# A graph kernel's edge sort: a running table in four classes of columns, table joins in three batches, and ranks by one comparison per step

## The chip, the cores and the metric

The kernel runs on one core of one Trainium2 chip. The time is that of one execution on the device in microseconds, the median of several runs. The core's engines are TensorE (PE in the profile; PEld is its weight load), VectorE (DVE), ScalarE (ACT), GpSimd (POOL) and SyncE (SP, which only issues DMAs here). Each takes its own instructions in order and waits for the others by semaphores.

## What is computed

A graph of 6250 nodes with 128 features and 100,000 edges goes through two layers, each followed by a residual sum and a layer norm. The edges come sorted by their destination, not by their source.

```python
# layer 0: attention over edges, 8 heads of 16
q, k, v = (x @ W.T + b for W, b in ((Wq, bq), (Wk, bk), (Wv, bv)))
scores = sum(q[src] * k[dest], per head) / sqrt(16) + attention_mask
weights = softmax of scores over the edges with the same src
out = segment_sum(v[src] * weights, dest) @ Wo.T + bo
# layer 1: a message per edge
h = silu(concat(x[src], x[dest], edge_features) @ eW1 + eb1)
agg = segment_sum(silu(h @ eW2 + eb2), src)
x = silu(concat(x, agg) @ nW1 + nb1) @ nW2 + nb2
```

The softmax runs over edges of one source, so the kernel first sorts the edges by source, on the chip.

## The kernel before

**Layout.** The edges stand in 784 columns of 128 (a column is one edge per partition). 16 columns make a step: 49 steps. The steps form three regions (`REG`): steps 0 to 8, steps 9 to 12, and the rest, the far region; the first two are the near regions, whose destinations are all in a narrow band. Each region is sorted on its own into a table `xs` in DRAM. A source node is a pair (block of 128 nodes, of which there are 49; place in the block).

**The counting sort.** `hist_steps` counts the edges of every node: for each column, a one-hot of the place (`lo1`, L229) times a one-hot of the block (`hi1`, L233) is accumulated on TensorE into `hist` (128 places x 49 blocks). `places` turns the counts of a region into the first position of each node (`st_b`: three parts whose sum is exact in bf16).

**One step of the sort** (loop at L897; its parts are interleaved by hand there, and a scheduler may move instructions further along each engine's queue, within the dependences). `prep_loads` issues the loads of the next step. `prep_hot` makes `hit` (L780, the one-hot of the place, transposed) and `lo1`, `hi1`. `prep_rank` makes `ohd` (L786) and the rank: how many edges with the same source stand earlier in the same column. `sk` holds, for each partition, the 127 keys before its own, for 16 columns; a comparison with the own key, with a sum, gives the rank of one column (L790), 16 times a step. `chain` (two halves of 8 columns) keeps the running table `base` in PSUM: how many edges of each node have passed. For each column, ScalarE copies `base` to `cs` (L805), TensorE adds the column to `base` (L806), and three matmuls with `hit` look up first position plus passed edges for the column's own nodes (`look`, L808). `pick` selects the right block (L822, L824); `send` adds the rank (L835), forms the position (L837) and scatters 8 columns, one indirect DMA each, from GpSimd (helper at L133). What is scattered is `stg`, a buffer of three copies, filled by `spread_k` (L817, the keys' projection spread by `ohd`) and `heads` (L828, L829). The first write to a copy (L828) waits until the scatters of three steps before have landed.

**Work beside the sort.** `between`, called after each half step, pulls a few pieces of other work: in steps 1 to 7 the histogram of the other regions and projections; at the end of step 7 `places` for regions 1 and 2; from step 9 on weights and projections, three pieces a time; then the near regions' scores, four pieces a time (`near_scores`, L704). That takes each near region's 16-column chunks from `xs` (fetch, turn, score, soft, stat: 14 pieces) and sums maxima and sums of exponentials per node into `stat_r`. At a region's end the sums are joined into `near_o`: for 4 blocks at a time, transposes (L725), a reduction (L728), and `pooled` (L692), which merges maxima and sums; each group is one piece. Behind the last region's joins `stat_r` is cleared (L739).

**Behind the sort.** `fast` (L939) handles the far region in the same way, reading `xs` from its first load on, then computes messages (scatters into `xmsg`), sums by destination, and runs layer 1.

Of the kernel before, what the change touches and what calls it, by code (L numbers as in the profile page):

```python
# [18 lines left out]
P = 128  # L19
# [13 lines left out]
AC = sum(AS)  # L33
BC = NC - AC
AT = AC * UC
REG = ((0, 9), (9, 4), (AC, BC))
KEYS = ((0, AS[0]), (AS[0], NC - AS[0]))
WT = (2, 1, 8)
# [20 lines left out]
def tile_gnn(  # L59
# [120 lines left out]
    def bank():  # L180
        return gps.tile([P, 512], F32, name="ps")
# [34 lines left out]

    def halves(r):
        cs = slice(KEYS[r][0] * UC, (KEYS[r][0] + KEYS[r][1]) * UC)
        part = ks.tile([P, 2, KEYS[r][1] * UC], I32, name=f"part{r}")
        nc.vector.tensor_single_scalar(part[:, 0], kc[r], P - 1, ALU.bitwise_and)  # L220
        nc.vector.tensor_copy(lo_c[:, cs], part[:, 0])
        nc.vector.tensor_single_scalar(part[:, 1], kc[r], 7, ALU.logical_shift_right)
        nc.vector.tensor_copy(hi_c[:, cs], part[:, 1])

    def onehots(c, pool, bufs=None):

# [118 lines left out]
            yield  # L345

    kps = sort.enter_context(tc.tile_pool(name="ksetp", bufs=1, space=PSUM))
    hist = kps.tile([P, len(REG), NB], F32, name="hist")
# [12 lines left out]

    def places(r):

        cnts.append(kp.tile([P, NB], F32, name=f"cnt{r}"))
        nc.vector.tensor_copy(cnts[r], hist[:, r, :])
        sums = bank()[:, :3 * NB].rearrange("p (a b) -> p a b", b=NB)
        nc.tensor.matmul(sums[:, 0, :], ones_f, cnts[r], start=True, stop=True)
        nc.tensor.matmul(sums[:, 1, :], after, cnts[r], start=True, stop=True)

        many = kp.tile([P, 1], F32, name=f"many{r}")  # L370
        nc.vector.tensor_reduce(many, cnts[r], AX.X, ALU.max)
        nc.vector.tensor_single_scalar(many, many, float(2 * P), ALU.is_gt)
# [6 lines left out]
        st_i = kp.tile([P, 4, NB], I32, name=f"st_i{r}")  # L379
        nc.vector.tensor_add(st_i[:, 3, :], pre[r], sums[:, 1, :])  # L380
        nc.vector.tensor_scalar(st_i[:, 0, :], st_i[:, 3, :], 9, 9, ALU.logical_shift_right, ALU.logical_shift_left)
        nc.vector.tensor_single_scalar(st_i[:, 1, :], st_i[:, 3, :], 510, ALU.bitwise_and)
        nc.vector.tensor_single_scalar(st_i[:, 2, :], st_i[:, 3, :], 1, ALU.bitwise_and)
        st_b.append(kp.tile([P, 3, NB], BF16, name=f"st_b{r}"))
        nc.vector.tensor_copy(st_b[r], st_i[:, :3, :])
# [306 lines left out]
    def pooled(o, z, sp, nwin, k):  # L692

        m, s = z[:, :, :, 0:8], z[:, :, :, 8:16]
        d = sp.tile([P, nwin, k, 8], F32, name=f"pd{k}{nwin}")
        nc.vector.tensor_scalar(d, s, 0.0, -BIG, ALU.is_equal, ALU.mult)
        nc.vector.tensor_add(d, d, m)
        nc.vector.tensor_reduce(o[:, :, 0:8], d.rearrange("p w k h -> p w h k"), AX.X, ALU.max)
        nc.vector.tensor_sub(d, d, o[:, :, None, 0:8].to_broadcast([P, nwin, k, 8]))
        nc.scalar.activation(d, d, AF.Exp)  # L700
        nc.vector.tensor_mul(d, d, s)
        nc.vector.tensor_reduce(o[:, :, 8:16], d.rearrange("p w k h -> p w h k"), AX.X, ALU.add)

    def near_scores():  # L704

        for r in range(FAR):
            with ExitStack() as own:
# [13 lines left out]
                for j0 in range(0, NB, 4):  # L721
                    m = min(4, NB - j0)
                    x = bank()
                    for i in range(m):
                        nc.tensor.transpose(x[:, i * 96:(i + 1) * 96],  # L725
                                            sums_of["src"][:96, (j0 + i) * P:(j0 + i + 1) * P], ident[:96, :96])
                    z = sp.tile([P, 4, 3, 16], F32, name="z3")
                    nc.vector.tensor_reduce(z[:, :m, 0:2].rearrange("p w a v -> p w (a v)"),  # L728
                                            x[:, :m * 96].rearrange("p (w k v) -> p w v k", k=3, v=32), AX.X, ALU.add)
                    o = sums_of["near"][:, j0:j0 + m]  # L730
# [4 lines left out]
                    some = sp.tile([P, 4, 8], F32, name="some")  # L735
                    nc.vector.tensor_single_scalar(some[:, :m], o[:, :, 8:16], 0.0, ALU.is_gt)
                    nc.vector.tensor_mul(o[:, :, 0:8], o[:, :, 0:8], some[:, :m])
                    yield
        nc.vector.memset(sums_of["src"], 0.0)  # L739
        yield  # L740
# [6 lines left out]
    base = cps.tile([P, NB], F32, name="base")  # L747
    kreg, work = {}, {}

    def region(c):  # L750
# [32 lines left out]
    def prep_rank(c):  # L783
        w = work[c]
        w["ohd"] = bw.tile([P, UC, P], BF16, name="ohd")
        nc.vector.tensor_scalar(w["ohd"], w["drow"], iota_p, None, ALU.is_equal)  # L786
        w["rank"] = bw.tile([P, UC], F32, name="rank")
        for j in range(UC):
            junk = bw.tile([P, 127], BF16, name="junk")
            nc.vector.tensor_scalar(junk, w["sk"][:, :, j], meta[:, c * UC + j, 0:1], 0.0, ALU.is_equal, ALU.add,  # L790
                                    accum_out=w["rank"][:, j:j + 1])

    def chain(c, h):
        w = work[c]
        r, cr = region(c)
        if h == 0:
            w["stg"] = bw.tile([P, UC, XW], F32, name="stg", bufs=3)
            w["pos"] = bw.tile([P, UC], F32, name="pos")
            if cr == 0:
                nc.tensor.matmul(base, ident_b, st_b[r][:, 2, :], start=True, stop=False, skip_group_check=True)  # L800
        w["look"] = lps.tile([P, 8, NB], F32, name="look", bufs=2)
        for j in range(8 * h, 8 * h + 8):
            lo, hi = (w[k][:, j // 4, :, j % 4] for k in ("lo1", "hi1"))
            cs = bw.tile([P, NB], BF16, name="cs", bufs=4)
            nc.scalar.copy(cs, base)  # L805
            nc.tensor.matmul(base, lo, hi, start=False, stop=False, skip_group_check=True)  # L806
# [24 lines left out]
    def send(c, h):  # L831
        w, hs = work[c], slice(8 * h, 8 * h + 8)
        r, _ = region(c)
        pos = w["pos"][:, hs]
        nc.vector.tensor_add(pos, pos, w["rank"][:, hs])  # L835
        posi = bw.tile([P, 8], I32, name="posi", bufs=6)
# [1206 lines left out]
```

## Time and profile before

| | |
|---|---|
| median of 3 runs | 3164.53 us (3162.35 to 3166.09) |
| the profiled execution | 3162.1 us |
| its span, first to last instruction | 3160.3 us |
| first scatter of the sort starts | 50.5 us |
| last scatter of the sort ends | 1219.8 us |
| busy in the span | PE 2308.0, DVE 2085.9, ACT 870.7, POOL 2066.0 us |
| granted TensorE clock, 50 to 436, 436 to 1220, behind that | 0.67, 0.63, 0.87 |

In a line of a group of instructions stand the line of the kernel, engine, operation, tiles (written<-read) and count; after the bar the busy time in us and the mean of one in ns; after the next bar the engine's idle time just before these instructions, and what ended most of it ("issue" is a wait for nothing that the profile shows). In the timeline the columns are start, duration, engine, line, operation, and in brackets the idle time before it. In the view of waits they are the total, the number of waits and the longest.

### The profile page before, as it was taken

Reading aid. Unit: us, or ns where it says so; the run is one execution under the profiler, and the core shown is the slowest. Engines: PE = TensorE matmul, PEld = TensorE weight load, DVE = VectorE, ACT = ScalarE, POOL = GpSimd, SP = SyncE. Lnnn points to the kernel's source line nnn. Section 1 sums busy time; section 2 is a strip of 40 time slices with the busy share of each in tenths; the row PEclk is TensorE's granted clock in tenths of the full one; section 3 lists DMA queues with packets and bytes.
Section 4 is the critical chain, followed back from the end, with each engine's and each line's share of the span. In section 5 each row is a group of like instructions: output and inputs, shape, how many; then the busy total and the mean of one; then the engine's idle time right before and its main releaser. Section 6 shows DMA issues by size and latency. Waiting matters only on the chain. (4 is left out here: it accounts for less than half of the span.)

```text
span 3160.3 us, 64246 instructions
## 1 busy us (share of the span) xinstructions
PE 2308.0 (73%) x22329; PEld 1875.0 (59%) x22412; DVE 2085.9 (66%) x6242; ACT 870.7 (28%) x2740; POOL 2066.0 (65%) x1993
## 2 busy tenths in 40 slices
PE   7767875555656532667778768644987999999998
PEld 5555545445545521556667657543975777777776
DVE  8886447676788762667778768634994555555564
ACT  3324433233323311222222222100042333333333
POOL 3877776677667653255777775775037777777774
PEclk9666667666666655778888878776998999999999
DMA  7855768566648614555665665325845444444452
GB/s 233 185 155 149 201 196 251 160 215 210 182 134 253 198 49 125 157 161 142 178 177 171 179 181 149 90 80 193 294 142 152 133 134 122 125 114 129 133 160 61
DMA packets 480741, 509.83 MB, mean 161 GB/s; under 512 B 150742, under 2 KB 403465, under 8 KB 475798
## 3 DMA queue, kind: packets, MB, share of 16 engines
q1 hardware_dynamic: 378644, 341.49, 37.8%
q0 software_dynamic: 61952, 132.22, 13.6%
q10 hardware_dynamic: 39810, 31.91, 3.4%
q8 instruction: 179, 2.93, 0.4%
q14 instruction: 156, 1.28, 0.1%
HBM read 380.69 MB, written 124.69 MB: 160 GB/s over the span
## 5 line engine op out<-in xcount | busy, mean ns | idle before, releaser
L133 POOL DMA_INDIRECT xs<-stg,posi x784 | 832.1, 1061 | 381.6 <-issue 207.3
L133 POOL DMA_INDIRECT xmsg<-msg,at x576 | 594.5, 1032 | 341.2 <-issue 139.1
L125 POOL DMA_INDIRECT bt<-b_tab,dsti x576 | 572.5, 994 | 175.4 <-issue 136.7
L806 PE MATMUL base<-hi,lo 128*128 128x49 bf16 x784 | 169.0, 216 | 214.1 <-ACT cs L805 175.7
L790 DVE TENSOR_SCALAR_CACHE_REDUCE junk<-sk,meta 128x127 bf16<-128x127 int16 x784 | 303.2, 436 | 9.1 <-DMA sk<-skew 9.1
L1294 DVE TENSOR_TENSOR fe<-po,b_sb 128x512 f32<-128x512 f32 x196 | 135.2, 690 | 241.2 <-PE po L1292 235.0
L808 PEld LDWEIGHTS <-hit 128*128 128x128 bf16 x2352 | 142.3, 114 | 230.8 <-issue 208.8
L815 PE MATMUL kx<-kw,ohd 128*128 128x128 bf16 x2352 | 239.8, 267 | 29.8 <-ACT stg L817 24.4
L805 ACT CAST cs<-base 128x49 bf16<-128x49 f32 x784 | 160.5, 205 | 312.7 <-PE base L806 247.8
L815 PEld LDWEIGHTS <-ohd 128*128 128x128 bf16 x2352 | 196.3, 123 | 59.2 <-issue 37.4
L1292 PEld LDWEIGHTS po<-w_sb,ht 128*128 128x128 f32 x1568 | 204.8, 193 | 26.7 <-issue 5.2
L610 PEld LDWEIGHTS <-oht 128*128 128x128 bf16 x2352 | 189.0, 121 | 42.7 <-DVE oht L597 28.5
L1313 PE MATMUL ps<-ohf,fe 128*128 128x128 f32 x1568 | 208.6, 276 | 6.8 <-ACT fe L1295 6.8
L1292 PE MATMUL po<-w_sb,ht 128*128 128x128 f32 x1568 | 210.9, 277 | 2.0 <-ACT ht L1286 0.7
L1313 PEld LDWEIGHTS ps<-ohf,fe 128*128 128x128 f32 x1568 | 191.1, 192 | 8.1 <-ACT fe L1295 8.0
L1295 ACT ACTIVATE fe<-fe 128x512 f32<-128x512 f32 x196 | 123.5, 630 | 230.9 <-DVE fe L1294 230.7
L808 PE MATMUL look<-st_b,hit 128*128 128x49 bf16 x1568 | 159.3, 206 | 35.2 <-DVE sel L822 27.5
L1154 PE MATMUL ps<-ohd,mt 128*128 128x128 f32 x1152 | 135.1, 280 | 66.2 <-DMA mt<-xmsg 61.7
L1286 ACT ACTIVATE ht<-pre 128x512 f32<-128x512 f32 x196 | 116.7, 596 | 241.0 <-PE pre L1282 221.9
L1154 PEld LDWEIGHTS ps<-ohd,mt 128*128 128x128 f32 x1152 | 132.7, 196 | 68.7 <-issue 60.2
L996 PE MATMUL qv<-vw,oht 128*128 128x128 bf16 x1728 | 137.7, 229 | 33.8 <-DVE msg L999 25.1
L610 PE MATMUL qv<-qw,oht 128*128 128x128 bf16 x1728 | 147.0, 255 | 18.1 <-DVE oht L597 13.7
(317 smaller groups left out, 5124.2 us busy)
## 6 DMA issues: line engine op xcount, KB each, us to landing
st<-xs SPq DMA_DIRECT2D x49, 1128.0 KB
srow<-slo_row SPq DMA_DIRECT2D x85, 512.0 KB
lob<-lob_row SPq DMA_DIRECT2D x49, 512.0 KB
drow<-dlo_row SPq DMA_DIRECT2D x49, 512.0 KB
sk<-skew SPq DMA_DIRECT2D x49, 508.0 KB
qw<-q_tab SPq DMA_DIRECT2D x208, 96.0 KB
aw<-a_tab SPq DMA_DIRECT2D x208, 96.0 KB
mt<-xmsg ACTq DMA_DIRECT2D x18, 1024.0 KB
```

The costliest lines, as they stand in the source:

```text
L125: nc.gpsimd.indirect_dma_start(out=dst, out_offset=None, in_=table, in_offset=bass.IndirectOffsetOnAxis(ap=idx, axis=0))
L133: apart(nc.gpsimd.indirect_dma_start(out=table, out_offset=bass.IndirectOffsetOnAxis(ap=idx, axis=0), in_=src, in_offset=None), group)
L610: nc.tensor.matmul(qe[:, i, :], w["oh"][:, 4 * q + i, :], w["qw"][:, (4 * q + i) // WT[r] % 8, k, :], start=(k == 0), stop=(k == 2))
L790: nc.vector.tensor_scalar(junk, w["sk"][:, :, j], meta[:, c * UC + j, 0:1], 0.0, ALU.is_equal, ALU.add, accum_out=w["rank"][:, j:j + 1])
L805: nc.scalar.copy(cs, base)
L806: nc.tensor.matmul(base, lo, hi, start=False, stop=False, skip_group_check=True)
L808: nc.tensor.matmul(w["look"][:, j - 8 * h, :], w["hit"][:, j, :], tab, start=(i == 0), stop=(i == 2))
L815: nc.tensor.matmul(kx[:, i, :], w["ohd"][:, 4 * q + i, :], w["kw"][:, q, a, :], start=(a == 0), stop=(a == 2))
L996: nc.tensor.matmul(ve[:, i, :], w["oh"][:, 4 * q + i, :], w["vw"][:, (4 * q + i) // WT[r], k, :F], start=(k == 0), stop=(k == 2))
L1154: nc.tensor.matmul(ps, mt[:, 4 * q + i, :], oh[:, i, :], start=(i == 0), stop=(i == 3))
L1292: nc.tensor.matmul(po[:, i, :], ht[:, i, :], cw["w2"], start=(i == 0), stop=(i == 3))
L1313: nc.tensor.matmul(ps[:, t % max(4, wt) // wt, :], fe_[:, t % 4, :], oh[:, t % 4, :], start=(t % wt == 0), stop=(t % wt == wt - 1))
```

## The change

- **Four classes.** Column j of a step belongs to class j mod 4. `hist` and `base` get 4 x 49 columns, one table per class; `st_b` holds a first position per node and class (a node's edges of class 0 first, then class 1, ...). The chain copies `base` once per 4 columns, adds the four columns to it, and then looks them up.
- **Ranks.** All 16 columns of `sk` are compared with the own keys in one operation, in place; the 127 rows are folded onto 63, then on 32, by two additions, and one sum over the rest gives the ranks.
- **Joins.** The reductions L728 stay in groups of 4 blocks, a piece each; `pooled` and what follows run for 17, 17 and 15 blocks, from a pool of their own, with single copies of their buffers. A region's join is 17 pieces now, 13 before.
- **Small ones.** `posi` has 8 copies for 6; `halves` uses one scratch tile.

```diff
-                nc.tensor.matmul(hist[:, r, :], lo1[:, t // 4, :, t % 4], hi1[:, t // 4, :, t % 4],
-                                 start=(c == 0 and t == 0), stop=(c == c0 + n - 1 and t == UC - 1),
+                nc.tensor.matmul(hist[:, t % KT, :], lo1[:, t // 4, :, t % 4], hi1[:, t // 4, :, t % 4],
+                                 start=(c == c0 and t == 0), stop=(c == c0 + n - 1 and t == UC - 1),
                                  skip_group_check=True)
+            if c == c0 + n - 1:
+                classes[r] = ks.tile([P, KT, NB], F32, name="classes", bufs=2)
+                nc.vector.tensor_copy(classes[r], hist)
...
-        nc.vector.tensor_copy(cnts[r], hist[:, r, :])
+        nc.vector.tensor_reduce(cnts[r], classes[r].rearrange("p k b -> p b k"), AX.X, ALU.add)
...
+        st_f = ks.tile([P, KT, NB], F32, name="st_f")
+        nc.vector.tensor_add(st_f[:, 0, :], pre[r], sums[:, 1, :])
+        for k in range(1, KT):
+            nc.vector.tensor_add(st_f[:, k, :], st_f[:, k - 1, :], classes[r][:, k - 1, :])
+        st_i = ks.tile([P, 4, KT, NB], I32, name="st_i")
+        nc.vector.tensor_copy(st_i[:, 3], st_f)
...
+                for b0 in range(0, NB, 17):
+                    nb = min(17, NB - b0)
+                    z = sp.tile([P, 17, 3, 16], F32, name="z3", bufs=1)
+                    for j0 in range(b0, b0 + nb, 4):
...
+                        yield
+                    o = sums_of["near"][:, b0:b0 + nb]
                     if r:
-                        nc.vector.tensor_copy(z[:, :m, 2], o)
-                    pooled(o, z[:, :m, :3 if r else 2], sp, m, 3 if r else 2)
+                        nc.scalar.copy(z[:, :nb, 2], o)
+                    pooled(o, z[:, :nb, :3 if r else 2], sp, nb, 3 if r else 2)
...
+        sk = w["sk"]
+        own = bw.tile([P, 1, UC], I16, name="own")
+        nc.vector.tensor_copy(own[:, 0, :], meta[:, c * UC:(c + 1) * UC, 0])
+        nc.vector.tensor_tensor(sk, sk, own.to_broadcast([P, 127, UC]), ALU.is_equal)
+        nc.vector.tensor_add(sk[:, 0:63, :], sk[:, 0:63, :], sk[:, 64:127, :])
+        nc.vector.tensor_add(sk[:, 0:32, :], sk[:, 0:32, :], sk[:, 32:64, :])
         w["rank"] = bw.tile([P, UC], F32, name="rank")
-        for j in range(UC):
-            junk = bw.tile([P, 127], BF16, name="junk")
-            nc.vector.tensor_scalar(junk, w["sk"][:, :, j], meta[:, c * UC + j, 0:1], 0.0, ALU.is_equal, ALU.add,
-                                    accum_out=w["rank"][:, j:j + 1])
+        nc.vector.tensor_reduce(w["rank"], sk[:, 0:32, :].rearrange("p k j -> p j k"), AX.X, ALU.add)
...
-        for j in range(8 * h, 8 * h + 8):
-            lo, hi = (w[k][:, j // 4, :, j % 4] for k in ("lo1", "hi1"))
-            cs = bw.tile([P, NB], BF16, name="cs", bufs=4)
+        for j0 in range(8 * h, 8 * h + 8, KT):
+            cs = bw.tile([P, KT, NB], BF16, name="cs", bufs=4)
             nc.scalar.copy(cs, base)
-            nc.tensor.matmul(base, lo, hi, start=False, stop=False, skip_group_check=True)
-            for i, tab in enumerate((st_b[r][:, 0, :], st_b[r][:, 1, :], cs)):
-                nc.tensor.matmul(w["look"][:, j - 8 * h, :], w["hit"][:, j, :], tab, start=(i == 0), stop=(i == 2))
+            for j in range(j0, j0 + KT):
+                lo, hi = (w[k][:, j // 4, :, j % 4] for k in ("lo1", "hi1"))
+                nc.tensor.matmul(base[:, j - j0, :], lo, hi, start=False, stop=False, skip_group_check=True)
+            for j in range(j0, j0 + KT):
+                k = j - j0
+                for i, tab in enumerate((st_b[r][:, 0, k, :], st_b[r][:, 1, k, :], cs[:, k, :])):
+                    nc.tensor.matmul(w["look"][:, j - 8 * h, :], w["hit"][:, j, :], tab, start=(i == 0),
+                                     stop=(i == 2))
```

In the changed kernel these lines are: comparison L806, additions L807 and L808, sum L810, copy of `base` L823, matmul into `base` L826 and `look` L830, `pick` L845 and L847, `posi` L860, scatters L134.

More of the change, by code (lines that the diff above doesn't have):

```diff
@@ L35 @@
 AT = AC * UC
+KT = 4
 REG = ((0, 9), (9, 4), (AC, BC))
@@ L218, in halves @@
         cs = slice(KEYS[r][0] * UC, (KEYS[r][0] + KEYS[r][1]) * UC)
[L219 to L223, printed above, removed]
+        part = ks.tile([P, KEYS[r][1] * UC], I32, name=f"part{r}")
+        nc.vector.tensor_single_scalar(part, kc[r], P - 1, ALU.bitwise_and)
+        nc.vector.tensor_copy(lo_c[:, cs], part)
+        nc.vector.tensor_single_scalar(part, kc[r], 7, ALU.logical_shift_right)
+        nc.vector.tensor_copy(hi_c[:, cs], part)
     def onehots(c, pool, bufs=None):
@@ L347, in tile_gnn @@
     kps = sort.enter_context(tc.tile_pool(name="ksetp", bufs=1, space=PSUM))
-    hist = kps.tile([P, len(REG), NB], F32, name="hist")
+    hist = kps.tile([P, KT, NB], F32, name="hist")
+    classes = {}
     def hist_steps(r):
@@ L377, in places @@
         nc.vector.tensor_sub(pre[r], upto, sums[:, 0, :])
[L379 to L385, printed above, removed]
+        st_f = ks.tile([P, KT, NB], F32, name="st_f")
[4 more added lines that the diff above has]
+        nc.vector.tensor_copy(st_i[:, 3], st_f)
+        nc.vector.tensor_scalar(st_i[:, 0], st_i[:, 3], 9, 9, ALU.logical_shift_right, ALU.logical_shift_left)
+        nc.vector.tensor_single_scalar(st_i[:, 1], st_i[:, 3], 510, ALU.bitwise_and)
+        nc.vector.tensor_single_scalar(st_i[:, 2], st_i[:, 3], 1, ALU.bitwise_and)
+        st_b.append(kp.tile([P, 3, KT, NB], BF16, name=f"st_b{r}"))
+        nc.vector.tensor_copy(st_b[r], st_i[:, :3])
         few.append(kp.tile([P, 1], F32, name=f"few{r}"))
@@ L694, in pooled @@
         m, s = z[:, :, :, 0:8], z[:, :, :, 8:16]
-        d = sp.tile([P, nwin, k, 8], F32, name=f"pd{k}{nwin}")
+        d = sp.tile([P, max(nwin, 17 * (nwin > 2)), k, 8], F32, name=f"pd{k}{nwin > 2}", bufs=1 + (nwin < 3))[:, :nwin]
         nc.vector.tensor_scalar(d, s, 0.0, -BIG, ALU.is_equal, ALU.mult)
@@ L720, in near_scores @@
                     tell_path()
[L721 to L730, printed above, removed]
-                    if r:
-                        nc.vector.tensor_copy(z[:, :m, 2], o)
-                    pooled(o, z[:, :m, :3 if r else 2], sp, m, 3 if r else 2)
-                    some = sp.tile([P, 4, 8], F32, name="some")
-                    nc.vector.tensor_single_scalar(some[:, :m], o[:, :, 8:16], 0.0, ALU.is_gt)
-                    nc.vector.tensor_mul(o[:, :, 0:8], o[:, :, 0:8], some[:, :m])
+            with tc.tile_pool(name=f"join{r}", bufs=2, side="right") as sp:
+                for b0 in range(0, NB, 17):
+                    nb = min(17, NB - b0)
+                    z = sp.tile([P, 17, 3, 16], F32, name="z3", bufs=1)
+                    for j0 in range(b0, b0 + nb, 4):
+                        m = min(4, b0 + nb - j0)
+                        x = bank()
+                        for i in range(m):
+                            nc.tensor.transpose(x[:, i * 96:(i + 1) * 96],
+                                                sums_of["src"][:96, (j0 + i) * P:(j0 + i + 1) * P], ident[:96, :96])
+                        nc.vector.tensor_reduce(
+                            z[:, j0 - b0:j0 - b0 + m, 0:2].rearrange("p w a v -> p w (a v)"),
+                            x[:, :m * 96].rearrange("p (w k v) -> p w v k", k=3, v=32), AX.X, ALU.add)
+                        yield
+                    o = sums_of["near"][:, b0:b0 + nb]
+                    if r:
+                        nc.scalar.copy(z[:, :nb, 2], o)
+                    pooled(o, z[:, :nb, :3 if r else 2], sp, nb, 3 if r else 2)
+                    some = sp.tile([P, 17, 8], F32, name="some", bufs=1)
+                    nc.vector.tensor_single_scalar(some[:, :nb], o[:, :, 8:16], 0.0, ALU.is_gt)
+                    nc.vector.tensor_mul(o[:, :, 0:8], o[:, :, 0:8], some[:, :nb])
@@ L746, in tile_gnn @@
     lps = sort.enter_context(tc.tile_pool(name="blps", bufs=1, space=PSUM))
-    base = cps.tile([P, NB], F32, name="base")
+    base = cps.tile([P, KT, NB], F32, name="base")
     kreg, work = {}, {}
@@ L799, in chain @@
             if cr == 0:
-                nc.tensor.matmul(base, ident_b, st_b[r][:, 2, :], start=True, stop=False, skip_group_check=True)
+                nc.tensor.matmul(base, ident_b, st_b[r][:, 2], start=True, stop=False, skip_group_check=True)
         w["look"] = lps.tile([P, 8, NB], F32, name="look", bufs=2)
-        for j in range(8 * h, 8 * h + 8):
-            lo, hi = (w[k][:, j // 4, :, j % 4] for k in ("lo1", "hi1"))
-            cs = bw.tile([P, NB], BF16, name="cs", bufs=4)
+        for j0 in range(8 * h, 8 * h + 8, KT):
+            cs = bw.tile([P, KT, NB], BF16, name="cs", bufs=4)
             nc.scalar.copy(cs, base)
-            nc.tensor.matmul(base, lo, hi, start=False, stop=False, skip_group_check=True)
-            for i, tab in enumerate((st_b[r][:, 0, :], st_b[r][:, 1, :], cs)):
-                nc.tensor.matmul(w["look"][:, j - 8 * h, :], w["hit"][:, j, :], tab, start=(i == 0), stop=(i == 2))
+            for j in range(j0, j0 + KT):
[6 more added lines that the diff above has]
+                                     stop=(i == 2))
     def spread_k(c, q):
@@ L835, in send @@
         nc.vector.tensor_add(pos, pos, w["rank"][:, hs])
-        posi = bw.tile([P, 8], I32, name="posi", bufs=6)
+        posi = bw.tile([P, 8], I32, name="posi", bufs=8)
         nc.vector.scalar_tensor_tensor(posi, pos, few[r], stay[:, c * UC + 8 * h:c * UC + 8 * h + 8],
```

## The prediction

> **What bounds the kernel now.** I read the page first, then the groups of GpSimd's instructions between 40 and 1222 us, its waits there, and its timeline. The change touches only the sort, the loop over 49 steps of 16 columns that ends with the last scatter into `xs`. Everything behind it starts from that scatter: the loads of the far region read `xs`. So the question is when the last scatter ends (1219.8 us in the trace), and the 1940.5 us behind it I carry over unchanged.
>
> The group of the scatters, and GpSimd's five longest waits (columns: us in total, times, longest):
>
> ```profile
> L133 POOL DMA_INDIRECT xs<-stg,posi x784 | 832.1, 1061 | 381.6 <-issue 207.3 <-ACT cs L805 105.2 <-DMA xs<-stg,posi 16.2
> ```
>
> ```profile
> POOL xs L133 <- issue: 207.3, 614, 20.3
> POOL xs L133 <- ACT cs L805: 105.2, 50, 44.5
> POOL xs L133 <- DMA xs<-stg,posi: 16.2, 53, 0.3
> POOL xs L133 <- ACT v L669: 15.6, 2, 9.2
> POOL xs L133 <- ACT stg L828: 13.2, 3, 12.5
> ```
>
> See that 832.1 + 381.6 us is 1213.7: GpSimd does nothing but this from the start to 1219.8. Most waits are 0.30 us long, and these are the issue of the next scatter, not a wait for anybody. The timeline shows the undisturbed beat of 0.96 + 0.30 = 1.26 us:
>
> ```profile
> 1111.56 0.96 POOL L133 DMA_INDIRECT xs<-stg,posi  x1 [0.30 <-issue]
> 1112.82 0.96 POOL L133 DMA_INDIRECT xs<-stg,posi  x1 [0.30 <-issue]
> ```
>
> From the scatters' rows of the timeline I add up three parts between the first start (50.5) and the last end. **Beat:** 784 x 1.26 = 988 us, which no edit touches. **Real gaps** (what is over 0.30 us of idle): 102 us, none of it in steps 0 to 16, 81 us in steps 17 to 43, and one gap of 20 us in step 46. **Stretched scatters** (what is over 0.955 us of duration): 83 us. So in steps 0 to 16 GpSimd is already never hungry, although VectorE is 50 to 91% busy in the 100 us stretches there; the engines that the change relieves can give back at most the 102 us, and a little ahead of step 0.
>
> The stretch has an owner. 137 scatters that run beside a one-hot comparison (L229 or L233, two SBUF operands) are 62.8 us too long; 91 others beside L780, L786 or L597 15.1 us; 267 others beside the rank operation (L790) only 4.2 us:
>
> ```profile
> 104.11 2.05 POOL L133 DMA_INDIRECT xs<-stg,posi  x1 [0.31 <-ACT stg L829]
> 104.12 1.20 DVE L229 TENSOR_TENSOR lo<-iota_e,lo_c 128x2048 bf16<-128x2048 bf16 x1
> 105.25 0.54 DVE L824 TENSOR_REDUCE pos<-sel 128x8 f32<-128x392 f32 x1
> ```
>
> This scatter lasted through the whole of L229. With 88 L229 in that time, a pair L229+L233 (1.22 + 0.55 us) costs GpSimd 62.8 / 88 = 0.71 us.
>
> **The change, part by part.**
>
> *Four classes of columns.* Today each column is a round trip: ScalarE copies `base`, TensorE adds to it, and the next copy waits.
>
> ```profile
> 575.35 0.21 PE L806 MATMUL base<-hi,lo 128*128 128x49 bf16 x1 [0.17 <-ACT cs L805]
> ...
> 575.59 0.20 ACT L805 CAST cs<-base 128x49 bf16<-128x49 f32 x1 [0.29 <-PE base L806]
> ```
>
> The beat is 0.50 us, 16 per step: 8.0 us. After it there are 4 round trips. The copy of 196 columns is bounded by 0.205 us (L805, 49 columns) and 0.588 us (L817, 512): linearly 0.33 us. The other part of the beat is 0.30 us, plus three more matmuls that start some 0.07 us apart: about 0.85 us, x4 = 3.4 us. So the chain loses 4.6 us per step, and ScalarE 16 x 0.205 - 4 x 0.33 = 2.0 us of work. The matmuls on `look` are the same in number.
>
> *Ranks.* Off go 784 operations of 0.436 + 0.081 us (L790 and its accumulator read): 404.7 us, 8.3 us per step. On come per step: a copy of 16 keys (0.17, as L549); a comparison of 2032 int16; two additions of 1008 and 512 int16; a sum over 512 (0.67, as L614). No row has a two-operand int16 operation. Lower bound: L229's rate, 2048 bf16 in 1.22 us and 784 in 0.55, gives 1.2 + 0.68 + 0.40 = 2.3 us. [...] I take 2.3, since L229 is the nearest row: same form, a repeated operand, two bytes. So VectorE does 3.1 us in place of 8.3, and is relieved by 5.2 us per step. [...]
>
> But these three operations read two SBUF operands, like L229, and so hold up scatters, which L790 hardly did. At 0.71 us per 1.77 us of pair they cost 0.93 us per step; by a scatter's chance to meet one of 1.2, 0.68 and 0.40 us in a beat of 1.26 us, and half its length each time, 0.85. The program's order sets other work between the three, so they do not act as one block: I take 0.7 us, x48 = 34 us, less 4 for L790, **+30 us**. [...]
>
> *Places and histogram.* `places(0)` stands ahead of the first scatter and gets a copy and a sum of 196 (0.33 + 0.36), four additions in place of one (+0.6), a conversion (0.3) and longer integer operations (+0.7): +2.3 us. The first half-chain is 8 x 0.5 - 2 x 0.85 = 2.3 us shorter, and the ranks of step 0, which VectorE does between 37.6 and 43.8 us, 3 to 5 us shorter; part of this was in the shadow of the chain. **-2 us** (ends -6 and +3). For regions 1 and 2 `places` runs in step 7, where GpSimd has a queue: nothing; without that queue 2 x 2.3 us.
>
> *Joins.* 26 groups of eight small operations (L696 to L702, L736, L737: 0.18 to 0.24 us, each waiting on the last and once on ScalarE's exponential) become 6 batches of eight, at 0.3 to 0.58 us (by L822, 392 elements in 0.56), beside the same reductions L728. VectorE goes from 45 us to some 22, and the copy L732 (13, 2.4 us) moves to ScalarE. Step 46's gap of 20 us lies in just this work: while the joins and the 5.39 us memset L739 pass, L822 of step 46 stands behind them on VectorE. In the new order every position of the sort stands ahead of the last region's joins. What then stands late is the join itself: three batches of 9 us, one `z3`, and the memset, some 32 us behind the last position; the drain of GpSimd's last two steps, 40 us now, covers it. If only half a step is queued, the joins end 20 us behind the last scatter and hold VectorE's first work of the far region. I take **+4 us** (0 to +20).
>
> *Gaps.* Where do the 81 + 20 us go? They are gaps of 1 to 12 us in a step, when ScalarE, in order, holds this step's `cs` or the near region's copies (L669, L637) while GpSimd empties its queue; `stg` has three buffers, so ScalarE may run at most two steps ahead (its 166.7 us of wait at L828 is that back-pressure, and harmless). With 4.6 us less chain and 5.2 us less VectorE work per step, gaps under 5 us should close and longer ones lose 5 us or more: of the 19 gaps of over 0.1 us, that leaves about 25 us in steps 17 to 43, and half the 20. What stays is the near region's own latency: loads of `st`, `srow`, `s8` through DRAM. I take 102 to 40: **-62 us** (ends -30 and -95).
>
> **The sum**, against the profiled execution of 3162.1 us (span 3160.3 and 1.8 around it; the median of the runs shown, 3164.5, is 2.4 above): -2 + 30 + 4 - 62 = -30 us, so 3132 in that execution, and 3134 as a median.
>
> **Rivals.**
> 1. *The gaps stay* (slower). They may belong to the near scores' chain through DRAM, not to ScalarE and VectorE work: L613 waited 45.9 us for L610, `srow` and `lob` loads 44 us. Then only 20 us close, the stalls are paid in the saturated steps all the same, and the sum is -2 + 30 + 4 - 20 = +12: 3176. It decides where less than 32 us of gaps closes. Against it: 46 us of the 102 are gaps that end with `cs L805`, the shortened chain.
> [...]
> 3. *GpSimd's beat alone is left.* Gaps fall to 10 and stalls to +10: -2 + 10 - 92 = -84: 3080.
> 4. *A near tail* of 20 us instead of 4, with the rest as forecast: 3150; part of the forecast's range.
>
> **Chances.** Forecast with its tail 0.56 (own range 3105 to 3155), rival 1 0.17, rival 2 0.12, rival 3 0.15. A measurement of this kernel tells 0.2% (6.3 us) from no change. Faster: 0.49 of the forecast, all of rival 3, 0.02 of the others: 0.66. Same: 0.05 of the forecast and 0.06 of the rivals: 0.11. Slower: 0.23. Leaving out some 0.1 on each side, the range is 3085 to 3185.
>
> **What would show it.** In the profile after: scatters at 1.26 us with the last one ending near 1190 instead of 1219.8; L823's copies 196 per run at 0.33 us; the comparison L806 near 1.2 us (2.2 means rival 2); the scatters' mean of 1061 ns rising to about 1100; real gaps of some 40 us, none in step 46. The forecast is wrong if the mean passes 1140, if the gaps in steps 17 to 43 stay at 70 or more, or if the far region's first load does not follow within 3 us of the last scatter.

## The result, and the profile after

The changed kernel takes 3174.69 us (median of 20 runs, 3165.19 to 3185.04), the kernel before 3164.61 us beside it; the ratio is 1.0027, with a 95% interval of 1.0016 to 1.0038. It is slower by a quarter of a per cent, where 3134 us and a gain were forecast. The profiled execution took 3169.7 us (span 3167.5).

The group of the scatters in the changed kernel, GpSimd's waits between 40 us and the end of the sort (total, times, longest), and one row of VectorE's waits:

```profile
L134 POOL DMA_INDIRECT xs<-stg,posi x784 | 864.9, 1103 | 365.1 <-issue 196.4 <-ACT stg L851 46.4 <-DVE pos L847 46.3
```

```profile
POOL xs L134 <- issue: 196.4, 640, 1.5
POOL xs L134 <- ACT stg L851: 46.4, 2, 29.7
POOL xs L134 <- DVE pos L847: 46.3, 2, 46.0
POOL xs L134 <- ACT stg L840: 35.0, 16, 18.7
POOL xs L134 <- DMA xs<-stg,posi: 20.7, 68, 0.3
```

```profile
DVE posi L860 <- DMA xs<-stg,posi: 69.3, 19, 9.2
```

See three things. The mean scatter went from 1061 to 1103 ns: these are the stalls. Of GpSimd's real gaps, 46 us ended with a copy `cs` before and 15 with a write to `stg`; now it is 2 and 76 (L840, L851), the latter in few and long pieces. (The 44.5 us among the waits for `cs` before and the 46.0 for `pos` now are the wait ahead of the first scatter.) And VectorE, which hardly waited for a place in `posi` before (0.9 us in all), now waits 69 us for one: the positions L860 stand in its queue until scatters of four steps ago have landed.

From the rows of the scatters I add up, by steps, the real gaps (idle over 0.305 us; by this count the 102 us of the prediction are 98.6) and the stretch (duration over 0.955 us):

| | before | after |
|---|---|---|
| first scatter starts | 50.5 | 52.1 |
| gaps, steps 0 to 16 | 0.1 | 0.1 |
| gaps, steps 17 to 36 | 66.4 | 4.5 |
| gaps, steps 37 to 45 | 12.2 | 75.9 |
| gaps, steps 46 to 48 | 19.9 | 0.0 |
| stretch, all steps | 83.5 | 116.3 |
| end of step 36 | 930.7 | 905.2 |
| last scatter ends | 1219.8 | 1236.1 |
| from there to the end | 1940.5 | 1931.4 |

Up to step 36 the changed kernel is 25.5 us ahead, much as forecast. Then it loses 61.5 us in nine steps, and gets 19.7 back at the end. So the question is what happens in steps 37 to 45.

One of these gaps, in the changed kernel's timeline (start, duration, engine, line, operation, idle before):

```profile
1065.80 0.96 POOL L134 DMA_INDIRECT xs<-stg,posi  x1 [0.30 <-issue]
1068.21 0.23 DVE L860 SCALAR_TENSOR_TENSOR posi<-pos,few,stay 128x8 int32<-128x8 f32 x1 [5.68 <-DMA xs<-stg,posi]
1070.69 0.75 DVE L607 TENSOR_SCALAR oht<-srow,iota_p 128x2048 bf16<-128x2048 bf16 x1
...
1071.50 2.74 PE L620 MATMUL ps<-qw,oht 128*128 128x128 bf16 x24 [7.76 <-DVE oht L607]
...
1082.56 0.59 ACT L840 COPY stg<-kx 128x512 f32<-128x512 f32 x1 [6.27 <-PE kx L838]
1083.05 0.24 ACT L851 COPY stg<-meta 128x48 f32<-128x48 f32 x1
1083.42 0.96 POOL L134 DMA_INDIRECT xs<-stg,posi  x1 [16.67 <-ACT stg L851]
```

Read it from the bottom. GpSimd starts step 42 after 16.67 us of idle, because `stg` of step 42 has only just been filled. The fill waited for TensorE's `kx`; TensorE stood at L620, a matmul of the near region, and waited 7.76 us for its one-hot L607; L607 stood on VectorE behind the positions L860, which waited until the last scatter of step 41 had landed. By their count, the positions that waited there were those of step 45. VectorE held up step 42 in order to store what is needed 97 us later. That wait is 5.68 of the 16.67 us, so this one chain is a reading; the runs below test it.

### The profile page after: what moved, and what is told of

It is laid out like the page before. It is cut to its first block, busy times and chain, and to the rows that moved or that the text cites. A ratio compares the mean times of both kernels' runs of the same rounds, so it can differ in the third digit from the quotient of the medians.

```text
span 3167.5 us, 62249 instructions
## 1 busy us (share of the span) xinstructions
PE 2255.0 (71%) x22330; PEld 1850.2 (58%) x22412; DVE 1954.0 (62%) x4763; ACT 789.8 (25%) x2135; POOL 2096.9 (66%) x1993
## 5 line engine op out<-in xcount | busy, mean ns | idle before, releaser
L134 POOL DMA_INDIRECT xs<-stg,posi x784 | 864.9, 1103 | 365.1 <-issue 196.4
L134 POOL DMA_INDIRECT xmsg<-msg,at x576 | 594.2, 1032 | 335.9 <-issue 132.6
L838 PE MATMUL kx<-kw,ohd 128*128 128x128 bf16 x2352 | 221.8, 267 | 134.5 <-ACT stg L840 103.7
L620 PEld LDWEIGHTS <-oht 128*128 128x128 bf16 x2352 | 188.8, 121 | 82.5 <-DVE oht L607 55.4
L840 ACT COPY stg<-kx 128x512 f32<-128x512 f32 x196 | 114.1, 587 | 223.8 <-PE kx L838 205.8
L620 PE MATMUL qv<-qw,oht 128*128 128x128 bf16 x1728 | 147.3, 256 | 17.9 <-DVE oht L607 13.2
L231 DVE TENSOR_TENSOR lo<-iota_e,lo_c 128x2048 bf16<-128x2048 bf16 x98 | 119.1, 1216 | 64.2 <-PE hist L358 47.9
L1305 PE MATMUL pre<-oht,aw 128*128 128x512 bf16 (+2 forms) x769 | 148.5, 314 | 7.7 <-issue 7.5
L1019 PEld LDWEIGHTS <-oht 128*128 128x128 bf16 x1728 | 118.1, 104 | 45.7 <-issue 40.3
L1329 DVE TENSOR_TENSOR ohf<-iota_f,slo 128x512 f32<-128x512 f32 x196 | 134.4, 687 | 9.1 <-PE ps L1336 1.5
```

The costliest lines, as they stand in the source:

```text
L134: apart(nc.gpsimd.indirect_dma_start(out=table, out_offset=bass.IndirectOffsetOnAxis(ap=idx, axis=0), in_=src, in_offset=None), group)
L620: nc.tensor.matmul(qe[:, i, :], w["oh"][:, 4 * q + i, :], w["qw"][:, (4 * q + i) // WT[r] % 8, k, :], start=(k == 0), stop=(k == 2))
L838: nc.tensor.matmul(kx[:, i, :], w["ohd"][:, 4 * q + i, :], w["kw"][:, q, a, :], start=(a == 0), stop=(a == 2))
L1019: nc.tensor.matmul(ve[:, i, :], w["oh"][:, 4 * q + i, :], w["vw"][:, (4 * q + i) // WT[r], k, :F], start=(k == 0), stop=(k == 2))
L1305: nc.tensor.matmul(pre[:, i * wt:(i + 1) * wt, :], w["aw"][:, 4 * q // WT[r] + i, k, :], w["oh"][:, 4 * q + i * wt:4 * q + (i + 1) * wt, : ...
L1329: nc.vector.tensor_tensor(oh, iota_f[:, None, :].to_broadcast([P, 4, P]), slo[:, cs, None].to_broadcast([P, 4, P]), ALU.is_equal)
```

## The experiments

Ratios are to the kernel before on the same chip, with 95% intervals. Where an expectation says "once more", the first run of that kernel fell on a chip that took a third longer for everything; those runs are told at the end. The first theory, A, is the convoy just read; its rivals are that the near region's second class is itself too slow (B), that one place, the late load of its first keys, is the largest loss (C), and that the order of the queues rather than the wait is the harm (D).

**Sixteen `posi`.** `name="posi", bufs=8` becomes `bufs=16`.

> The changed kernel with 16 instead of 8 buffers for the positions `posi`. What is known: the changed kernel ends its scatters at 1236.1 us instead of 1219.8; up to step 36 it is 25.5 us ahead, in steps 37 to 45 it loses 61.5, in 76 us of real gaps. Theory A (a convoy over `posi`): VectorE runs four steps ahead with positions, fills all 8 `posi`, and then waits in order for a scatter to land (69 us at L860, 19 times), with the near region's operations queued behind it; TensorE waits for those, and the spread of the keys into `stg`, for which GpSimd waits, stands behind them. With 16 buffers that wait at L860 is under 10 us, the gaps of steps 40 to 44 fall from 46 to 15 us or less, the last scatter ends near 1205 and the time is 3140 to 3150. Theory B (the near region's second class is itself too slow: four chunks, each a chain of loads through DRAM, VectorE, TensorE and ScalarE, beside less than two steps of sort): the wait at L860 goes, but another one (TensorE on L620 or L691) takes its place; gaps in steps 37 to 45 stay at 65 to 85 us and the time at 3168 to 3180.

Measured: 3144.03 us, ratio 0.9922 (0.9902 to 0.9941). The last scatter ends at 1205.5, gaps are 49.0 us in all. VectorE's row of waits:

```profile
DVE posi L860 <- DMA xs<-stg,posi: 2.7, 11, 0.5
```

The wait is gone, and 31 us of gaps with it. B's sign, another wait in its place, is not there: between 905 and 1150 us TensorE's waits at L620 and L691 fell from 60 to 29 us. A holds, B does not. What is left are one gap of 29.8 us ahead of step 38 and one of 10.9 ahead of step 40.

**Four `posi`.** `bufs=8` becomes `bufs=4`.

> The changed kernel with 4 instead of 8 buffers for `posi`. Theory A: the wait for a free `posi` comes two steps sooner, so it is there in more of steps 17 to 45: 69 us at L860 or more, time 3175 to 3200. Theory D (the harm is not the wait but that the order of the queues lets the positions run four steps ahead of the spread of the keys, so that near work and the spread stand behind work that GpSimd does not need yet): with 4 buffers the order itself is tighter, positions lead by 20 to 40 us instead of 60 to 110, gaps in steps 37 to 45 fall from 76 to 40 us or less, and the time is 3130 to 3155.

Measured: 3197.92 us, ratio 1.0086 (1.0067 to 1.0106). Gaps 102.2 us, and

```profile
DVE posi L860 <- DMA xs<-stg,posi: 166.9, 42, 8.7
```

With 4, 8 and 16 buffers the wait is 167, 69 and 3 us and the ratio 1.0086, 1.0027 and 0.9922. D falls, A holds a second time, in the other direction.

**The first load of the second class early.** The load gets a buffer of its own and stands behind the start of the first class:

```diff
-                s["begin"]()
+                s["begin"](sums_of["s0f"] if r else None); r or firsts(sums_of["s0f"], xs[1][0:1, :])
```

> The changed kernel, in which the first load of the near region's second class (`s0f`, the first keys of its windows) is issued when the first class begins, into a buffer of its own, instead of behind the joins of the first class. Known: TensorE waits 19.0 us for it at 927 to 946 us, since the load stands on SyncE's queue behind two loads of the sort, whose buffers VectorE frees only behind a join and a memset of 5.39 us; GpSimd's gap ahead of step 38 is 29.7 us, the longest. Theory C (that place is the largest single loss): TensorE's wait for it is under 3 us, that gap 10 to 15 us, and the time 3155 to 3163. Theory B (the second class's own chain sets the pace of steps 37 to 45): that gap shrinks, but those of steps 40 to 44 grow by as much; the time stays at 3168 to 3180.

Measured: 3183.42 us, ratio 1.0029 (1.0009 to 1.0049): no gain, and 3 us above what B gave as well. TensorE's wait of 19.0 us for this load is gone from the trace, and GpSimd's gap ahead of step 38 is still there:

```profile
964.56 0.96 POOL L134 DMA_INDIRECT xs<-stg,posi  x1 [27.91 <-ACT stg L851]
```

The longest wait on TensorE was not what GpSimd waited for. C falls.

**The ranks as before.** L790's 16 comparisons with a sum in place of the new lines; classes, joins and 8 `posi` stay.

> The changed kernel with the ranks as before: 16 comparisons with a sum per step in place of one comparison, two additions and one sum; the four classes, the joins in three batches and 8 `posi` stay. By the forecast's terms: the stretch of the scatters falls from 116 us to 85 to 95, since the three two-operand int16 operations go, and VectorE has 5.2 us more per step. If VectorE's relief through the ranks is what lets positions run ahead (theories A and D), positions lead by less, the gaps in steps 37 to 45 fall below 50 us, while gaps in steps 17 to 36 come back to 20 to 60; time 3150 to 3175. If the late gaps belong to the near region's own chain (theory B) they stay at 65 to 85 us; time 3160 to 3185.

Measured: 3148.42 us, ratio 0.9937 (0.9916 to 0.9957). Stretch 87.5 us; gaps 50.7 in steps 17 to 36 and 12.4 in 37 to 45; no wait for `posi` (0.2 us). The time is 1.6 us below the range of A and D. So the new ranks made the change a loss. They cost stalls (29 us), and with them VectorE runs into its own buffers; they also close the gaps of steps 17 to 36 (50.7 to 4.5 us).

**The new ranks alone**, in the kernel before (six `posi`).

> The kernel before with the new ranks alone once more, for the same reason. Stalls of the scatters up by some 30 us, to about 115; gaps 60 to 90 us in place of 99, since the round trips of the running table stay; ratio to the kernel before 0.998 to 1.008. If VectorE's ranks were what the gaps waited for, gaps of 40 us and a ratio of 0.990 to 0.995.

Measured: 3235.09 us, ratio 1.0200 (1.0174 to 1.0226), well beyond what I expected: stretch 106.8 us, gaps 144.1, of which 21.1 in steps 17 to 36 (66.4 before) and 115.8 in 37 to 45. The expectation took it that the round trips of the running table hold the positions back. They run ahead all the same, to the end of their six buffers:

```profile
DVE posi L841 <- DMA xs<-stg,posi: 103.0, 25, 12.0
```

**Joins in groups of four again**, with 16 `posi`: in `near_scores`, `range(0, NB, 17)` becomes `range(0, NB, 4)`, with `z3`, `pd` and `some` of that size. What is left after the first run is the gap ahead of step 38. Theory J lays it to the batched joins; theory S to the three `stg`, which let the spread of the keys run no further than two steps ahead of the step being scattered, so that in ScalarE's and TensorE's order it stands behind the whole passage from the near region's first class to its second.

> The kernel with joins in groups of four and 16 `posi` once more, for the same reason. Theory J: the gap ahead of step 38 falls from 29.8 to 16 us or less, ratio to the kernel before 0.984 to 0.989. Theory S: the gap stays at 25 to 40 us, ratio 0.991 to 0.997.

Measured: 3159.66 us, ratio 0.9967 (0.9951 to 0.9982). The gap grew, and now stands ahead of step 37:

```profile
958.41 0.96 POOL L134 DMA_INDIRECT xs<-stg,posi  x1 [40.68 <-ACT stg L839]
```

J falls; the batches are a gain of their own, of about half a per cent here (18 us at the last scatter, 11 of them stretch).

**Four `stg`**, with 16 `posi`. A fourth copy needs room, so the one-hot `hit` is written over its input:

```diff
-        w["hit"] = bw.tile([P, UC, P], BF16, name="hit")
+        w["hit"] = w["lob"]
...
-            w["stg"] = bw.tile([P, UC, XW], F32, name="stg", bufs=3)
+            w["stg"] = bw.tile([P, UC, XW], F32, name="stg", bufs=4)
```

> The kernel of the run with four `stg` once more (16 `posi`, `hit` over `lob`), because the chip of that run took 4242 us for the kernel before, with stalls of up to 20 us all over the program, so that its microseconds don't stand beside those of the other runs. On a chip that takes 3160 to 3170 us for the kernel before: theory S (the spread of the keys may run only three steps ahead, and stands behind the change from the near region's first class to its second) gives gaps ahead of steps 38 and 40 of 10 us or less together (29.8 and 10.9 with three `stg`) and a ratio to the kernel before of 0.980 to 0.986. Theory J (the batched joins) leaves that gap at 20 us or more and the ratio at 0.988 to 0.993.

Measured: 3116.67 us, ratio 0.9827 (0.9801 to 0.9852), the last scatter ends at 1175.4. These are the only gaps over 2 us:

```profile
930.89 0.96 POOL L134 DMA_INDIRECT xs<-stg,posi  x1 [5.03 <-ACT stg L851]
985.42 1.02 POOL L134 DMA_INDIRECT xs<-stg,posi  x1 [10.25 <-ACT stg L840]
```

Together they are 15 us, more than the 10 I expected, but the ratio is where S put it. To see that the fourth buffer did it and not the one-hot in place, the next run keeps three `stg`.

> The changed kernel with 16 `posi`, three `stg` and `hit` over `lob` once more, for the same reason. If the fourth `stg` made the step from a ratio of 0.9922 to 0.9827: 0.990 to 0.995 and 40 to 60 us of gaps. If the in-place one-hot did: 0.981 to 0.986 and gaps under 25 us.

Measured: 3137.40 us, ratio 0.9924 (0.9906 to 0.9943), gaps 42.8 us: as with 16 `posi` alone. It was the buffer.

**The same buffers in the kernel before**: 16 `posi`, four `stg`, `hit` in place, and, for room, a pool of their own for its joins (their copy L732 then goes to ScalarE).

> The kernel before with 16 `posi`, four `stg` and `hit` over `lob` once more, because on the chip of that run the kernel before took 4304 us, with waits all over the program that no record explains. On a chip at 3160 to 3170 us: theory R (in the kernel before, too, the three `stg` are the limit): gaps from 99 to 35 us or less, ratio 0.977 to 0.984. Theory K (its gaps belong to the round trip of each column, and there is no lead for a buffer to hold): gaps 60 to 95 us, ratio 0.988 to 1.000.

Measured: 3082.58 us, ratio 0.9752 (0.9736 to 0.9768); gaps 12.4 us, the last scatter ends at 1139.5. The ratio is below even what R gave (0.977 to 0.984). R holds, and K, which is the prediction's own reading, falls: the gaps of the kernel before close with the same work, VectorE busy 815.4 us for 816.4 from the first scatter to the end of the last, ScalarE 379.1 for 375.0. The four edits were not run one by one in this kernel. It hardly waited for `posi`, `hit` in place did little in the changed one, and half of its gaps lie ahead of its first join (L728 from 868 us on), so the gain is put down mainly to the fourth `stg`; that is an argument, not a run.

**Old ranks, classes, joins and the buffers together**: the changed kernel with L790's ranks, 16 `posi`, four `stg`, `hit` in place, and for room three `cs` and one `junk`.

> The changed kernel with the ranks as before, and with 16 `posi` and four `stg` (three `cs` in place of four, for room). With the old ranks, 8 `posi` and three `stg` the ratio to the kernel before was 0.9937; its gaps (77 us, 51 of them in steps 17 to 36) do not show a wait for `posi`, and end mostly behind VectorE's and ScalarE's own work. If stalls (-30 us against the new ranks) and run-ahead add up, the ratio is 0.978 to 0.984 and the old ranks are the better ones; if VectorE's 4 to 5 us per step of rank work keep it from running ahead, four `stg` change nothing here: 0.990 to 0.996.

Measured: 3062.43 us, ratio 0.9645 (0.9619 to 0.9671): the best of all, and below the range expected. GpSimd has nothing left but its beat, 4.7 us of gaps and the stalls:

```profile
L134 POOL DMA_INDIRECT xs<-stg,posi x784 | 835.5, 1066 | 286.9 <-issue 191.5 <-DVE pos L843 43.9 <-DMA xs<-stg,posi 17.4
```

```profile
POOL xs L134 <- issue: 191.5, 628, 0.3
POOL xs L134 <- DVE pos L843: 43.9, 2, 43.6
POOL xs L134 <- DMA xs<-stg,posi: 17.4, 57, 0.3
POOL xs L134 <- ACT cs L819: 7.5, 10, 4.8
```

Against the run with four `stg` and the new ranks this gives the price of the ranks with the gaps out of the way: the first scatter 3.1 us earlier, 33.7 us less stretch, 10.1 us less gap, 46.9 us in all, by which the last scatter does end earlier (1128.5 for 1175.4). VectorE is busy 129 us longer in the sort in this kernel (816.3 us for 686.9), and GpSimd's gaps are shorter all the same. (Three `cs` for four and one `junk` are in the difference too.)

**Runs on two other chips.** Eight runs fell on two chips on which every kernel took a third longer (4242 and 4304 us for the kernel before), with 390 to 640 us of gaps. Five were kernels told above, and were made again for that reason. Of their ratios there: four `stg` 0.9613, joins of four 0.9680, ranks alone 0.9857, `hit` in place 0.9634, the kernel before with the buffers 1.0030. Three were made there alone. Without the two additions, the sum running over 2032 elements, 16 `posi` and three `stg`:

> The changed kernel with 16 `posi`, and the two additions taken out: the sum runs over all 127 comparisons of a column (2032 elements) instead of 32 (512). It measures what the two additions cost GpSimd. If every two-operand operation of 16-bit data from SBUF holds up the scatters beside it, the stretch falls from 117 us to 95 to 105 (the scatters beside L807 and L808 are 35 us too long together, in part through other operations); VectorE pays 1 to 3 us more per step for the longer sum. If the sum over strided int16 holds them up as well, the stretch stays at 112 to 125. The time follows the stretch where GpSimd has its queue: 3125 to 3140 in the first case, 3143 to 3160 in the second.

and with four:

> The changed kernel with 16 `posi` and four `stg`, in which GpSimd has no gaps to speak of (15 us) and 120.6 us of stretch, without the two additions: the sum runs over 2032 instead of 512 elements. If each two-operand operation holds up the scatters beside it, the stretch falls to 98 to 108 us, and the time with it: ratio to the kernel before 0.974 to 0.979 in place of 0.9827. If a sum over strided int16 holds them up too, or VectorE's longer sum brings gaps back, 0.981 to 0.988.

Measured: ratios 0.9801 and 0.9767, stretch 74.3 and 71.2 us, where the kernels with additions have 82.1 (ranks alone) to 93.7 (four `stg`) on such a chip. That the additions hold up scatters fits this; but GpSimd has no queue there, the two kernels of a pair were not always on one chip, and the time did not follow. The price of the additions alone stays open. The old ranks with three `stg`, 16 `posi` and `hit` in place:

> The kernel with the old ranks, 16 `posi` and three `cs` (ratio 0.9645 with four `stg`), with three `stg` instead of four, `hit` still over `lob`. If the fourth `stg` is what took its gaps from 77 to 5 us, the ratio is 0.988 to 0.995 and gaps are 50 to 80 us. If the place of `hit` or the `cs` did it, 0.964 to 0.972.

Measured: 0.9864 (0.9818 to 0.9911), gaps 571 us; nothing follows for the other chips.

## Why the prediction was wrong

**What bounds the kernel: right.** The end of the sort is GpSimd's last scatter. The far region's first load follows it by 1.9 us (1238.0 after 1236.1), and the time behind it is within what the runs told above differ by (1930.5 to 1941.5 us).

**The sizes of the work: right for single operations, wrong for VectorE's relief.** L823 comes 196 times at 0.323 us (0.33 forecast), four columns take 0.77 us of round trip (0.85). The comparison L806 takes 1.20 us (1.2), the additions 0.67 and 0.41 (0.68, 0.40); only the sum L810 takes 1.06 in place of 0.67. The relief of 5.2 us per step was about twice too large. The prediction added up the records of L790, 404.7 us, but they lie over each other. Of the kernel before:

```profile
562.58 0.43 DVE L790 TENSOR_SCALAR_CACHE_REDUCE junk<-sk,meta 128x127 bf16<-128x127 int16 x1
562.94 0.07 DVE L790 DVE_READ_ACCUMULATOR junk<-sk,meta 128x1 f32 x1
562.94 0.43 DVE L790 TENSOR_SCALAR_CACHE_REDUCE junk<-sk,meta 128x127 bf16<-128x127 int16 x1
```

The next comparison starts 0.36 us after the last, beside the accumulator read. So L790 keeps VectorE busy for 304.6 us, 6.2 per step and not 8.3, and the new lines for 172.9 us, 3.5 per step. From the first scatter to the end of the last VectorE is busy 816.4 us before and 686.3 after, 2.7 us less per step, and ScalarE 375.0 and 294.4, 1.6 per step. For this comparison the choice of L229's rate held: 2032 int16 in 1.20 us are 0.59 ns each, and L229's 2048 bf16 in 1.215 us are 0.59 too.

**Stalls: right.** +33 us of stretch, +30 forecast. Of the changed kernel's timeline:

```profile
179.01 2.04 POOL L134 DMA_INDIRECT xs<-stg,posi  x1 [0.30 <-DVE own L805]
179.02 1.19 DVE L806 TENSOR_TENSOR sk<-sk,own 128x2032 int16<-128x2032 int16 x1
```

The scatter is 1.08 us too long, the comparison beside it lasts 1.19. A fit of all scatters' excess against the time that each lay beside each line of VectorE gives L806 27 us, L807 and L808 some 5 each; this is an estimate, not a run.

**Start and tail: small.** The first scatter comes 1.6 us later, for -2. The joins are done before the last scatter (by 1200 us), so nothing of the +4 came, nor the fourth rival's 20 us, and step 46 has no gap, as forecast. With 32.8 us of stretch and -18.2 of gaps that is the last scatter's +16.3 us. Behind it the two profiled executions differ by -9.1 us, no more than the runs do, so the span is 7.2 us longer; the medians differ by 10.1.

**Gaps: here it failed.** -62 was forecast, -18 came (98.6 to 80.4). The step was "With 4.6 us less chain and 5.2 us less VectorE work per step, gaps under 5 us should close and longer ones lose 5 us or more". It took every gap for a lack of speed per step. In steps 17 to 36 less work did close them (66.4 to 4.5 us, with half the relief forecast on VectorE). In steps 37 to 45 they grew from 12.2 to 75.9, so that 72.2 us stand in steps 17 to 43, over the 70 that the prediction itself named as a sign of being wrong. There speed was not short: with the same work and the larger buffers (16 `posi`, four `stg`) these steps have 14.7 us. A step's `stg` and positions are made in the same queues as near-region work that comes in blocks (the longest, the passage between its two classes, keeps the spread from 887 to 955 us), and what carries GpSimd over a block is the steps finished beforehand. How many these can be is set by the buffers, and a wait for a free one holds up all that stands behind it in the queue. The kernel before with more buffers and no less work shows it (gaps 98.6 to 12.4).

The prediction had the row in hand and called it wrong: "its 166.7 us of wait at L828 is that back-pressure, and harmless". Of the kernel before:

```profile
593.35 0.24 ACT L828 COPY stg<-meta 128x48 f32<-128x48 f32 x1 [13.46 <-DMA xs<-stg,posi]
...
594.22 0.21 PE L806 MATMUL base<-hi,lo 128*128 128x49 bf16 x1 [13.45 <-ACT cs L805]
...
605.87 1.63 POOL L133 DMA_INDIRECT xs<-stg,posi  x1 [8.64 <-ACT cs L805]
```

While ScalarE waits for a free `stg`, the copies `cs` stand behind it, TensorE waits for them as long, and GpSimd runs dry at the next half step. In the second halves of steps 23 to 35 the spread is 23 us or more ahead of its scatter, but the positions, in all but one, only 0.7 or 0.8; with the buffers they are 7 to 23 us ahead, and the waits at that write come to 66.0 us. By these rows, the wait for `stg` held up the positions ahead of the change, and the wait for `posi` holds up the spread after it. The prediction named no wait at `posi` at all, though its eight buffers stood in the list of changes: with less work VectorE reached that end, and what queued behind the wait was the work that GpSimd needed.

Why did steps 17 to 36 go well, and 37 to 45 not? In steps 17 to 36 positions come 1 to 53 us ahead of their scatter and the spread up to 38; from step 38 on the positions are 60 to 110 us ahead, at the end of their eight buffers, and the spread of steps 38, 40, 42 and 44 0.3 us. The passage between the near region's classes (joins, the 5.39 us memset, the first loads) uses up the lead of the spread, and after it every wait at `posi` falls on a spread that is late. Sixteen `posi` take away the second (49.0 us of gaps are left), and the fourth `stg` most of the first (14.8).

**The rivals.** The first, "the gaps stay", gave 3176 with the condition that less than 32 us of gaps closes. Time and condition came true (18 us); its reason, the near scores' own chain through DRAM, did not, since the gaps close with that chain untouched; that its time is right is chance. The second, with 2.2 us for L806 and 3180 us, rests on a slower rate for int16 that no run shows: L806 took 1.20 us. The third, GpSimd's beat alone, was no outcome of this change, but is what the buffers give: with them and the old ranks the last scatter ends 91 us earlier than before.

**What stays open.** Why the order of the queues puts the spread behind the passage, the scheduler's part in it, wasn't tried. That 16 `posi` and four `stg` are the fewest that do it wasn't, either. The classes and joins with the buffers (0.9645) against the kernel before with the buffers (0.9752) come to about 1.1% by the ratios, made on two chips; the traces show 11 us of it at the last scatter, but only 4 over the whole span, so its size is open.

## What to carry to other kernels

Before gaps on the bounding engine are put down to slow feeders, compare how far ahead of their use the feeders finish; where an in-order engine waits for a buffer at one time and is late at another, what stands behind the wait may be late because of it, and more buffers can close the gaps without less work (here 98.6 to 12.4 us, with VectorE busy 815.4 us for 816.4). When a change frees an in-order engine, ask which of its writes will first wait for a free buffer (here `posi`, 0.9 to 69.3 us of wait), and what is queued behind it. And an operation that holds up the bounding engine can be dear even where it saves its own engine much: here 129 us less on VectorE cost 47 us at the last scatter.

## What the runs showed of the hardware

On two of the five chips on record (the result's own is not) the same kernels took a third longer. ScalarE's operations have the lengths of the others there (`cs` 0.205 us in both; between 100 and 430 us the mean of all is 0.430 us there without the additions, and 0.433 in the changed kernel's profile), but all engines wait at many places for causes that no record shows: with the new ranks alone, between 100 and 430 us, waits for which the profile names no instruction last up to 16.9 us on GpSimd, 12.7 on TensorE, 20.5 on ScalarE and 16.3 on VectorE. In the kernel before with the buffers the profile names nothing that ended 136 of ScalarE's waits of over 3 us, 920 us in all, where the same kernel on another chip has one such wait, of 4.8 us. The mean granted clock is lower there (0.70 to 0.73, for 0.78 to 0.80); whether that is a cause of the waits or comes of them stays open.

There GpSimd is not saturated (390 to 640 us of gaps), and the order turns round: with 16 `posi`, `hit` in place and three `stg` the new ranks give 0.9634 and the old (with three `cs`) 0.9864, while on another chip, with four `stg`, the new ranks lose 1.8%. So an edit that pays on one chip need not pay on another.
